# A four-layer graph network on one core: attention scores scaled and summed by one VectorE operation each, row sums moved to GpSimd, one copy in halves

## The chip, the cores and the metric

The kernel runs on one core of a Trainium2 chip. The metric is the time of one execution on the device in microseconds (us), smaller is better. PE is TensorE (the matrix multiplier), PEld its weight loads, DVE is VectorE, ACT is ScalarE, POOL is GpSimd, SP is the engine whose queue issues the DMAs.

## The reference

Input are 128 graphs of 128 nodes with 512 features in fp32, `x` of (128, 128, 512), and one weighted adjacency matrix per graph, `adj` of (128, 128, 128). Four layers follow each other; each adds its result to `x` and normalizes the rows (mean and variance over the 512 features):

```
x = LN(x + relu(An @ x @ W0 + b0))          An = d * (A + I) * d,  d = rowsum(A + I) ** -0.5
qk = x @ Wqk.T ;  q, k = halves of 64
w  = softmax over nodes of ( rowsum( (q @ k.T) / sqrt(64) * A ) )
x = LN(x + w * (x @ Wv.T))
x = LN(x + relu([x, (A @ x) / max(rowsum(A), 1e-6)] @ W2.T))
x = LN(x + An @ (x @ W3 + b3))
```

The second layer matters here. The row sum of masked scores needs no full score matrix: row n of it is the dot product of `q[n]` with `(A @ k)[n]`, over 64 elements, times 1/8. The kernel holds A with its rows divided by `dm = max(rowsum(A), 1e-6)`, so it multiplies by `dm` to undo that. The softmax over the 128 nodes of a graph gives one weight per node.

The fourth layer's bias, seen through An, is `b3` times a row sum of An for each node: `rs = d * (dm * (A_divided @ d) + d)`.

## The kernel before

The 128 graphs are worked in 32 tiles of G = 4 graphs; within a tile a graph's 128 nodes lie on the 128 partitions. Every dense product of a layer (`project`, `l1_out`) is a 2 by 2 block product done with seven instead of eight block products, named B11, T1, B21, T2, B22, T3 and T4 (in this order on PE in layer 3); sums of left-hand blocks are made by `left_sums`, mostly on GpSimd, sums of products on VectorE. In the steady state one turn of the main loop works on two tiles: tile t is in layers 0 and 1, tile u = t - 1 in layers 2 and 3:

```python
        l1_out(t, {})
        l3_agg(u)
        l1_scores(t)
        l3_bias(u)
        l3_out(u, {B11: [lambda: l1_softmax(t)], B21: [lambda: l1_add(t)]})
```

The hooks in braces are called after the named block product. So PE's order is: the products of layer 1 (`p_v`), the four aggregations of layer 3 (`p_agg`, written `agg3` by ACT copies), the four small products of `l1_scores` (`p_sc`, 64 columns for the scores and one for the row sums of each graph), block product B11 of layer 3, the transpose `p_w` of the summed scores, T1, B21, the transpose `p_ws` of the softmax weights back to nodes, then T2, B22 and so on.

Between `p_sc` and `p_ws` stands the softmax. `l1_scores` multiplies on VectorE the PSUM tile `p_sc` by q (two operations of 128 elements into `scr`), sums each graph's 64 products (`w`), and multiplies by 1/8 and `dm` (`w` again). Then it makes `rs` in three operations of 4 elements; `rs` isn't used before `l3_bias` in the next turn. `l1_softmax` transposes `w` on PE to 4 rows of 128, takes the maximum (`mx`), negates it (`nmx`), exponentiates on ACT (`e`, with its sum `ssum`), and normalizes on VectorE (`rsum`, `e`). `l1_add` transposes `e` back (`p_ws`), copies it (`ws`), and adds `ws` times the values to `x`.

`l3_bias` adds `b3` times `rs` to `x` of tile u, one VectorE operation of 512 elements per graph.

The order of the instructions on each engine is not that of the program. The program is recorded as operations in `Plan`; the order on PE is kept, and that of the other four engines is made by a list schedule. It takes, of what is ready, the operation with the earliest due time (counted back from PE's order), with the durations that `estimate` gives. `estimate` also says by a fourth value, `port`, whether an operation may not overlap with another such: every GpSimd operation has it, and VectorE operations with two inputs in SBUF of more than 32 elements. All records have line L271 in the profile, since one line emits every instruction; they are told apart by tile names.

Of the kernel before, what the change touches and what calls it, by code (L numbers as in the profile page):

```python
# [10 lines left out]
FP = mybir.dt.float32  # L11
AF = mybir.ActivationFunctionType
ALU = mybir.AluOpType
AX = mybir.AxisListType

P = 128
K = 32
Q = P // K
G = 4
F = 512  # L20
C = F // P
H = F // 2
ATT = 64
V = H + ATT
# [267 lines left out]
def estimate(engine, method, args, kw):  # L292

    out = args[0]
    n = out.idx.size if isinstance(out, Ref) else 0
    if engine == "tensor":
        return (max(109, 0.85 * n) if method == "transpose" else 2 * max(104, 0.833 * n + (2.5 if n > P else 5))), 100, 0, False
    if method == "dma_start":
        size = max(int(np.prod(v.shape)) if isinstance(v, bass.AP) else v.idx.size * 32 * len(v.quads) for v in args)
        return 470, Plan.LAND + size / 60, size, False  # L300
    if engine == "scalar":
        return (380 if method == "activation" else 160) + 0.83 * n, 0, 0, False
    if engine == "gpsimd":
        return (400 + 150 * n if ALU.pow in args else 250 + 2 * n), 0, 0, True
    if method in ("bn_stats", "tensor_reduce"):
        n = args[1].idx.size
    both = [v for v in args[1:] if isinstance(v, Ref) and v.idx.size == n and v.tile.args[3]["tag"] not in ("pb", "pt")]
    return 160 + (1.12 if len(both) > 1 else 1.04) * n, 0, 0, len(both) > 1 and n > 32


@with_exitstack
def kernel(
# [11 lines left out]
    out: bass.AP,  # L324
):
    nc = Plan(tc.nc, estimate)
    B = x.shape[0]
    NT = B // G
# [5 lines left out]
    tp = Pool(nc, ctx.enter_context(tc.tile_pool(name="tp", bufs=4)), 4)  # L334
    sp = Pool(nc, ctx.enter_context(tc.tile_pool(name="sp", bufs=4)), 4)
# [7 lines left out]
    st = {}  # L343
# [41 lines left out]
    p = ps_t.tile([P, C, P], FP, tag="pt", name="p_warm")  # L385
# [21 lines left out]
    def per_graph(v):  # L407
        return v[:, :, None].to_broadcast([P, G, P])


    def prep_rows(t):
        ana = st["ana", t]
        a = ana[:, 1]
        deg = sp.tile([P, G], FP, tag="deg", name=f"deg_{t}")
        nc.vector.tensor_reduce(deg, a, AX.X, ALU.add)
        dh = sp.tile([P, G], FP, tag="dh", name=f"dh_{t}")
        nc.vector.tensor_scalar(dh, deg, 1.0, None, ALU.add)
        d = sp.tile([P, G], FP, tag="d", name=f"d_{t}")
        nc.gpsimd.tensor_tensor(d, dh, nhalf, ALU.pow)
        dm = sp.tile([P, G], FP, tag="dm", name=f"dm_{t}")  # L420
        nc.vector.tensor_scalar(dm, deg, DEG_EPS, None, ALU.max)
        rdeg = sp.tile([P, G], FP, tag="rdeg", name=f"rdeg_{t}")
        nc.vector.reciprocal(rdeg, dm)
        nc.vector.tensor_tensor(ana[:, 0], a, ident[:, None, :].to_broadcast([P, G, P]), ALU.add)
        nc.vector.tensor_tensor(ana[:, 0], ana[:, 0], per_graph(d), ALU.mult)
        nc.vector.tensor_tensor(ana[:, 1], a, per_graph(rdeg), ALU.mult)
        st["d", t], st["dm", t] = d, dm

    def prep_tiles(t):
        st["anT", t] = ap.tile([P, G, P], FP, tag="anT", name=f"anT_{t}", bufs=3)  # L430
# [29 lines left out]
    def left(name, t):  # L460
        st[name, t] = tp.tile([P, G, C, P], FP, tag="left", name=f"{name}_{t}")

    def aggregate(name, t, g, aT):

        xin = st["x", t]
        p = ps_t.tile([P, C, P], FP, tag="pt", name=f"p_{name}_{t}_{g}")
        with nc.unit():
            for c in range(C):
                nc.tensor.matmul(p[:, c, :], xin[:, g, c * P:(c + 1) * P], aT[:, g, :], start=True, stop=True)
        nc.scalar.copy(st[name, t][:, g], p)  # L470

    def turn_x(name, t, r):

# [26 lines left out]
    def left_sums(name, t, eng=nc.gpsimd, pairs=(slice(0, 2),)):  # L500

        a = st[name, t].rearrange("p (q r) (h c) n -> p q r h c n", r=2, h=2)
        s = [tp.tile([P, 2, 2, P], FP, tag=f"s{i}", name=f"{name}s{i}_{t}", bufs=3) for i in (1, 2, 4)]
        for q in pairs:
            a11, a12, a21, a22 = a[:, q, 0, 0], a[:, q, 0, 1], a[:, q, 1, 0], a[:, q, 1, 1]
            s1, s2, s4 = (v[:, q] for v in s)
            eng.tensor_tensor(s1, a21, a22, ALU.add)
            eng.tensor_tensor(s2, s1, a11, ALU.subtract)
            eng.tensor_tensor(a21, a11, a21, ALU.subtract)
            eng.tensor_tensor(s4, a12, s2, ALU.subtract)  # L510
        st[name, t] = {B11: a[:, :, 0, 0], B21: a[:, :, 0, 1], B22: s[2], T4: a[:, :, 1, 1], T1: s[0], T2: s[1],
                       T3: a[:, :, 1, 0]}
# [170 lines left out]
    def l1_scores(t):  # L683


        d, dm = st["d", t], st["dm", t]
        p = ps_t.tile([P, G, ATT + 1], FP, tag="pt", name=f"p_sc_{t}")
        with nc.unit():
            for g in range(G):
                nc.tensor.matmul(p[:, g, :], st["arT", t][:, g, :], st["v", t][g % 2, 1][:, g // 2, H:V + 1],  # L690
                                 start=True, stop=True)
        w = sp.tile([P, G], FP, tag="w", name=f"w_{t}")
        scr = tp.tile([P, F], FP, tag="row", name=f"scr_{t}", bufs=1)[:, 0:G * ATT].rearrange("p (g a) -> p g a", g=G)
        for r in range(2):
            nc.vector.tensor_tensor(scr.rearrange("p (q r) a -> p q r a", r=2)[:, :, r],
                                    p.rearrange("p (q r) a -> p q r a", r=2)[:, :, r, 0:ATT],
                                    st["v", t][r, 0][:, :, H:V], ALU.mult)
        nc.vector.tensor_reduce(w, scr, AX.X, ALU.add)
        nc.vector.scalar_tensor_tensor(w, w, 1.0 / ATT ** 0.5, dm, ALU.mult, ALU.mult)
        rs = sp.tile([P, G], FP, tag="rs", name=f"rs_{t}")  # L700
        nc.vector.tensor_tensor(rs, p[:, :, ATT], dm, ALU.mult)
        nc.vector.tensor_tensor(rs, rs, d, ALU.add)
        nc.vector.tensor_tensor(rs, rs, d, ALU.mult)
        st["w", t], st["rs", t] = w, rs

    def l1_softmax(t):
        p = ps_t.tile([P, P], FP, tag="pt", name=f"p_w_{t}")
        nc.tensor.transpose(p[:G, :], st.pop(("w", t)), ident)
        mx = sp.tile([G, 1], FP, tag="mx", name=f"mx_{t}")
        nc.vector.tensor_reduce(mx, p[:G, :], AX.X, ALU.max)  # L710
        nmx = sp.tile([G, 1], FP, tag="nmx", name=f"nmx_{t}")
        nc.vector.tensor_scalar(nmx, mx, -1.0, None, ALU.mult)
        e = sp.tile([G, P], FP, tag="e", name=f"e_{t}", bufs=1)
        ssum = sp.tile([G, 1], FP, tag="ssum", name=f"ssum_{t}")
        nc.scalar.activation(e, p[:G, :], AF.Exp, bias=nmx, scale=1.0, accum_out=ssum)
        rsum = sp.tile([G, 1], FP, tag="rsum", name=f"rsum_{t}")
        nc.vector.reciprocal(rsum, ssum)
        nc.vector.tensor_scalar(e, e, rsum, None, ALU.mult)
        st["e", t] = e
# [94 lines left out]
    def l3_agg(t):  # L814
        left("agg3", t)
        for g in (0, 1, 3, 2):
            aggregate("agg3", t, g, st["anT", t])
        left_sums("agg3", t)

    def l3_agg_pair(t, q, eng):  # L820
# [27 lines left out]
    def begin():  # L848

        prep_rows(0)  # L850
        prep_transpose(0)
        weight_sums(w0_sb, nc.gpsimd)
        l0_agg(0, nc.vector, ONE_BY_ONE)
        prep_rows(1)
        l0_out(0, {B21: [lambda: prep_transpose(1)], B22: [lambda: l0_agg(1)]})
        weight_sums(wv_sb, nc.vector)
        for w in (w2x_sb, w2a_sb, w3_sb):
            weight_sums(w, nc.gpsimd)

        l0_out(1)  # L860
        l1_turn(0, turn_on_tensor, (0,))
        finish_tails()
        l1_turn(0, turn_on_tensor, (1,))
        l1_out(0, {T3: [lambda: l1_turn(1, turn_on_tensor)]})
        l1_out(1, {B11: [lambda: l1_scores(0)], T1: [lambda: l1_softmax(0)], B21: [lambda: l1_add(0)]})
        l2_both(0, 0)
        l2_out(0, {B21: [lambda: l2_both(0, 1), lambda: prep(2)], T2: [lambda: l1_scores(1)], B22: [lambda: l1_softmax(1)], T3: [lambda: l1_add(1)]})
        l0_agg(2)
        l2_turn(1)
        l0_out(2, {B21: [lambda: l2_agg(1, 0)], T1: [lambda: l2_agg(1, 1)]})  # L870
        l3_agg(0)
        l3_bias(0)
        l3_out(0)

    def prep(t):
        if t < NT:
            load(t)
            prep_rows(t)
            prep_turn(t)
# [60 lines left out]
```

## Time and profile before

| | |
|---|---|
| time, median of 3 | 2489.15 us (2488.21 to 2489.63) |
| profiled execution | 2489.66 us, of which the profile's span 2487.9 us |
| busy: PE, PEld | 2443.3 us (98%), 2087.7 us (84%) |
| busy: DVE, ACT, POOL | 1792.9 us (72%), 990.7 us (40%), 1302.7 us (52%) |
| one turn of the main loop, 1017.0 to 1093.4 us | 76.4 us, PE busy 75.68 us in it |
| granted TensorE clock | 0.998 |

"Busy" is the time in which an engine has an instruction under way. An idle time is put down in the profile to the instruction whose end released the waiting one. The profile's chain is followed back from the last instruction, each step to what released it. [...]

### The profile page before, as it was taken

How to read it: one execution, taken by the hardware profiler on the slowest of the kernel's cores; microseconds unless marked ns; L12 is line 12 of the kernel's file. 1: busy time of each engine (PE TensorE's matmuls, PEld its weight loads, DVE VectorE, ACT ScalarE, POOL GpSimd, SP SyncE). 2: the span in 40 equal slices, each digit the busy share in tenths (PEclk: the TensorE clock that was granted, in tenths of full speed). 3: DMA queues.
4: the chain of work that ended last, by engine and by line, in shares of the span. 5: the costliest groups of instructions: out<-in, count | busy, mean ns of one | idle time of the engine just before them, and what ended most of it. 6: DMA issues, size and time to landing. Idle time of an engine off the chain costs nothing.

```text
span 2487.9 us, 35407 instructions
## 1 busy us (share of the span) xinstructions
PE 2443.3 (98%) x12462; PEld 2087.7 (84%) x12462; DVE 1792.9 (72%) x3357; ACT 990.7 (40%) x2057; POOL 1302.7 (52%) x1522
## 2 busy tenths in 40 slices
PE   8999999999999999999999999999999999999998
PEld 7788888888888888888888888888888888888886
DVE  6677776877767777677776767767687676877665
ACT  3344334443334443343433444333444334444335
POOL 5365555545455454555554554645555455545443
PEclk9999999999999999999999999999999999999999
DMA  5143234442334423244332444233443334432220
GB/s 174 26 123 80 77 102 110 123 104 61 106 99 123 123 63 100 84 123 123 83 92 82 114 123 107 70 99 94 123 123 72 86 89 123 123 96 64 81 71 34
DMA packets 393265, 241.14 MB, mean 97 GB/s; under 512 B 140416, under 2 KB 358016, under 8 KB 393088
## 3 DMA queue, kind: packets, MB, share of 16 engines
q1 hardware_dynamic: 393088, 238.88, 35.7%
q8 instruction: 99, 1.62, 0.3%
q14 instruction: 78, 0.64, 0.1%
HBM read 126.62 MB, written 112.20 MB: 96 GB/s over the span
## 4 chain that ended last, share of the span: by engine, by line
PE 90%; DVE 7%; ACT 1%; issue 1%; DMA 1%; SPq 0%; POOL 0%; ACTq 0%; POOLq 0%; DVEq 0%
PE p_o L271 55%; PE p_v L271 19%; PE p_agg L271 14%; DVE x L271 2%; DVE rs L271 2%; DVE w L271 1%; PE p_sc L271 1%; DVE scr L271 1%; ACT e L271 1%; DMA x<-in_x_dram 0%; SPq L271 0%; DVE e L271 0%; DVE mx L271 0%; PE p_ws L271 0%; DVE rsum L271 0%
## 5 line engine op out<-in xcount | busy, mean ns | idle before, releaser
L271 PE MATMUL p_o<-w_sb,agg 128*128 128x256 f32 x2048 | 471.5, 380 | 1.7 <-DVE u_o L271 1.0
L271 PEld LDWEIGHTS p_o<-w_sb,agg 128*128 128x128 f32 x2048 | 385.9, 190 | 54.0 <-ACT s_o L271 1.1
L271 ACT COPY agg<-p_agg 128x512 f32<-128x512 f32 x384 | 221.0, 583 | 450.4 <-PE p_agg L271 450.4
L271 PE MATMUL p_v<-wv_sb,xT 128*128 128x320 f32 x1024 | 291.4, 432 | 0.0
L271 DVE TENSOR_TENSOR v<-p_v,v 128x320 f32<-128x320 f32 x316 | 154.7, 490 | 173.2 <-PE p_v L271 172.1
L271 PE MATMUL p_o<-w2x_sb,xT 128*128 128x256 f32 x1024 | 263.3, 379 | 1.7 <-ACT s_o L271 1.1
L271 PE MATMUL p_o<-w2a_sb,agg 128*128 128x256 f32 x1024 | 262.8, 379 | 0.0
L271 PEld LDWEIGHTS p_v<-wv_sb,xT 128*128 128x128 f32 x1024 | 192.1, 190 | 75.9
L271 PEld LDWEIGHTS p_agg<-anT,x 128*128 128x128 f32 x2048 | 238.7, 192 | 6.9 <-DVE anT L271 0.4
L271 PE MATMUL p_agg<-anT,x 128*128 128x128 f32 x2048 | 239.4, 275 | 0.2 <-DVE anT L271 0.2
L271 POOL TENSOR_TENSOR xT1s<-xT 128x512 f32<-128x512 f32 x32 | 45.5, 1423 | 346.0 <-DVE xT L271 230.0
L271 PEld LDWEIGHTS p_o<-w2x_sb,xT 128*128 128x128 f32 x1024 | 194.1, 190 | 32.6 <-ACT s_o L271 1.9
L271 PE MATMUL p_v<-wv_sb,xT1s 128*128 128x320 f32 x768 | 217.4, 433 | 0.1
L271 PEld LDWEIGHTS p_o<-w2a_sb,agg 128*128 128x128 f32 x1024 | 194.6, 190 | 26.4
L271 DVE TENSOR_TENSOR u_o<-p_o,u_o 128x512 f32<-128x512 f32 (+1 forms) x196 | 131.1, 670 | 118.4 <-PE p_o L271 118.2
L271 ACT ACTIVATE x<-x,nmro,rstdo 128x512 f32<-128x512 f32 x257 | 198.7, 809 | 4.3
L271 PE MATMUL p_o<-w2x_sb,xT2s 128*128 128x256 f32 x768 | 197.3, 379 | 1.5 <-DVE xT2s L271 1.5
L271 PE MATMUL p_o<-w2a_sb,agg2s 128*128 128x256 f32 x768 | 197.1, 379 | 0.0
L271 PEld LDWEIGHTS p_v<-wv_sb,xT1s 128*128 128x128 f32 x768 | 145.7, 190 | 57.7 <-POOL xT1s L271 0.6
L271 PE MATMUL p_o<-w_sb,agg0s 128*128 128x256 f32 x768 | 178.6, 382 | 4.3 <-DVE u_o L271 2.7
L271 ACT ACTIVATE nmro<-mro 128x2 f32<-128x2 f32 (+1 forms) x131 | 26.7, 204 | 389.6 <-POOL mro L271 389.6
L271 PE MATMUL p_o<-w_sb,agg3s 128*128 128x256 f32 x744 | 173.8, 383 | 0.0
(144 smaller groups left out, 4426.1 us busy)
## 6 DMA issues: line engine op xcount, KB each, us to landing
x<-in_x_dram SPq DMA_DIRECT2D x31, 1024.0 KB, 5.6
out_dram<-x SPq DMA_DIRECT2D x31, 1024.0 KB, 5.2
xT2s<-x SPq DMA_DIRECT2D x120, 256.0 KB, 2.5
xT2y<-xT2s SPq DMA_DIRECT2D x240, 128.0 KB, 3.3
xT1s<-x SPq DMA_DIRECT2D x120, 256.0 KB, 2.6
xT1y<-xT1s SPq DMA_DIRECT2D x240, 128.0 KB, 3.2
sa<-ana SPq DMA_DIRECT2D x120, 128.0 KB, 3.5
ya<-sa SPq DMA_DIRECT2D x120, 128.0 KB, 2.7
```

What stands on the lines that cost most here:

```text
L271: getattr(getattr(self.nc, op.engine), method)(*[v.real() if isinstance(v, Ref) else v for v in args], **{k: v.real() if isinstance(v, Ref ...
```

## The change

Five edits:

- `l1_scores` makes `w` by four `scalar_tensor_tensor` operations, one per graph, which multiply 64 elements of `p_sc` by a scalar per node and by q, and sum the products in the same instruction (`accum_out`). The scalar is `dmn = -dm / 8`, made for each tile on ACT in `prep_rows`. So `w` is the negative of what it was.
- `l1_softmax` takes the minimum (`mn`) in place of the maximum, and ACT computes exp(mn - w) with scale -1. The negation `nmx` is gone.
- The last two of the three operations on `rs` go to GpSimd.
- `estimate` sets `port` for VectorE operations with two SBUF inputs of any size.
- `l3_agg` copies the aggregation of its last graph (g = 2) from PSUM in two operations of 256 elements in place of one of 512.

```diff
-    return 160 + (1.12 if len(both) > 1 else 1.04) * n, 0, 0, len(both) > 1 and n > 32
+    return 160 + (1.12 if len(both) > 1 else 1.04) * n, 0, 0, len(both) > 1
...
+        dmn = sp.tile([P, G], FP, tag="dmn", name=f"dmn_{t}")
+        nc.scalar.mul(dmn, dm, -1.0 / ATT ** 0.5)
...
-    def aggregate(name, t, g, aT):
+    def aggregate(name, t, g, aT, parts=1):
...
-        nc.scalar.copy(st[name, t][:, g], p)
+        for c in range(0, C, C // parts):
+            nc.scalar.copy(st[name, t][:, g, c:c + C // parts], p[:, c:c + C // parts])
...
-        scr = tp.tile([P, F], FP, tag="row", name=f"scr_{t}", bufs=1)[:, 0:G * ATT].rearrange("p (g a) -> p g a", g=G)
-        for r in range(2):
-            nc.vector.tensor_tensor(scr.rearrange("p (q r) a -> p q r a", r=2)[:, :, r],
-                                    p.rearrange("p (q r) a -> p q r a", r=2)[:, :, r, 0:ATT],
-                                    st["v", t][r, 0][:, :, H:V], ALU.mult)
-        nc.vector.tensor_reduce(w, scr, AX.X, ALU.add)
-        nc.vector.scalar_tensor_tensor(w, w, 1.0 / ATT ** 0.5, dm, ALU.mult, ALU.mult)
+        scr = tp.tile([P, F], FP, tag="row", name=f"scr_{t}", bufs=1)
+        for g in range(G):
+            nc.vector.scalar_tensor_tensor(scr[:, g * ATT:(g + 1) * ATT], p[:, g, 0:ATT], st["dmn", t][:, g:g + 1],
+                                           st["v", t][g % 2, 0][:, g // 2, H:V], ALU.mult, ALU.mult,
+                                           accum_out=w[:, g:g + 1])
         rs = sp.tile([P, G], FP, tag="rs", name=f"rs_{t}")
         nc.vector.tensor_tensor(rs, p[:, :, ATT], dm, ALU.mult)
-        nc.vector.tensor_tensor(rs, rs, d, ALU.add)
-        nc.vector.tensor_tensor(rs, rs, d, ALU.mult)
+        nc.gpsimd.tensor_tensor(rs, rs, d, ALU.add)
+        nc.gpsimd.tensor_tensor(rs, rs, d, ALU.mult)
...
-        mx = sp.tile([G, 1], FP, tag="mx", name=f"mx_{t}")
-        nc.vector.tensor_reduce(mx, p[:G, :], AX.X, ALU.max)
-        nmx = sp.tile([G, 1], FP, tag="nmx", name=f"nmx_{t}")
-        nc.vector.tensor_scalar(nmx, mx, -1.0, None, ALU.mult)
+        mn = sp.tile([G, 1], FP, tag="mn", name=f"mn_{t}")
+        nc.vector.tensor_reduce(mn, p[:G, :], AX.X, ALU.min)
...
-        nc.scalar.activation(e, p[:G, :], AF.Exp, bias=nmx, scale=1.0, accum_out=ssum)
+        nc.scalar.activation(e, p[:G, :], AF.Exp, bias=mn, scale=-1.0, accum_out=ssum)
...
     def l3_agg(t):
-            aggregate("agg3", t, g, st["anT", t])
+            aggregate("agg3", t, g, st["anT", t], 2 if g == 2 else 1)
```

## The prediction

> **What bounds the kernel now.** I read the page's busy shares and its chain first. PE is busy for 2443.3 of 2487.9 us, so all its idle time, start and end included, is 44.6 us. Nothing in this change makes PE's own work shorter, so that is the ceiling. The chain says which engine stands in PE's way:
>
> ```profile
> PE 2443.3 (98%) x12462; PEld 2087.7 (84%) x12462; DVE 1792.9 (72%) x3357; ACT 990.7 (40%) x2057; POOL 1302.7 (52%) x1522
> ...
> PE 90%; DVE 7%; ACT 1%; issue 1%; DMA 1%; SPq 0%; POOL 0%; ACTq 0%; POOLq 0%; DVEq 0%
> ```
>
> DVE carries 7% of the chain although it is no bottleneck by its busy time. The waits of PE alone name the place:
>
> ```profile
> PE p_ws L271 <- DVE e L271: 22.3, 31, 0.7
> PE p_o L271 <- DVE u_o L271: 3.8, 3, 2.7
> PE p_o L271 <- ACT s_o L271: 1.8, 3, 0.7
> ```
>
> Half of PE's idle time is one wait: in 31 of 32 tiles the transpose `p_ws` waits for the softmax weights `e`, never more than 0.73 us. All other waits come a few times, at the start and the end of the program. So in the steady state PE waits for nothing else. The timeline of VectorE in one turn (start, duration, instruction) shows the chain between `p_sc`, which ends at 1043.39, and `p_ws`:
>
> ```profile
> 1043.41 0.49 DVE L271 TENSOR_TENSOR scr<-p_sc,v 128x128 f32<-128x128 f32 x2 [0.91 <-PE p_sc L271]
> 1043.93 0.42 DVE L271 TENSOR_REDUCE w<-scr 128x4 f32<-128x256 f32 x1
> 1044.39 0.61 DVE L271 SCALAR_TENSOR_TENSOR w<-w,dm 128x4 f32<-128x4 f32 x1
> 1044.92 0.15 DVE L271 TENSOR_TENSOR rs<-p_sc,dm 128x4 f32<-128x4 f32 x1
> 1045.11 1.24 DVE L271 TENSOR_TENSOR rs<-rs,d 128x4 f32<-128x4 f32 x1
> 1046.27 1.83 DVE L271 SCALAR_TENSOR_TENSOR x<-b_sb,rs,x 128x512 f32<-128x512 f32 x1
> 1048.02 0.27 DVE L271 TENSOR_REDUCE mx<-p_w 4x1 f32<-4x128 f32 x1
> 1048.33 0.14 DVE L271 TENSOR_SCALAR nmx<-mx 4x1 f32<-4x1 f32 x1
> ```
>
> Two rows stand out: 1.24 us for 4 elements, where the fastest instruction of the same kind took 0.12, and 1.83 us where the fastest took 0.74. GpSimd's timeline tells why:
>
> ```profile
> 1045.06 1.27 POOL L271 TENSOR_TENSOR agg3s<-agg,agg3s 128x512 f32<-128x512 f32 x1
> 1046.28 1.27 POOL L271 TENSOR_TENSOR agg<-agg 128x512 f32<-128x512 f32 x1
> ```
>
> The first ended together with the GpSimd sum beside it (1046.34 and 1046.33), the second, which came as the next sum began, 0.55 us after that sum. And PE's:
>
> ```profile
> 1046.98 1.89 PE L271 MATMUL p_o<-w_sb,agg 128*128 128x256 f32 x8
> 1049.59 0.19 PE L271 MATMUL p_ws<-ident,e 4*128 4x4 f32 x1 [0.72 <-DVE e L271]
> ```
>
> PE is through with B21 at 1048.87 and stands for 0.72 us. `e` ends 6.07 us after `p_sc` here and, by the same timelines, within 0.4 us of that in all turns of the main loop; `p_ws` could go at about 5.3. So the bound is one chain, late by 0.72 us per turn, and its worst part isn't softmax work but `rs` and the bias of another tile, blocked by GpSimd.
>
> **What the Trainium skill says.** "SBUF — State Buffer", section "SBUF: two separate sides": a VectorE instruction with two SBUF inputs and a GpSimd instruction that reads SBUF exclude each other, each for its whole length. The trace agrees (0.12 against 1.24 us); `rs<-p_sc,dm` and `scr`, with one input in PSUM, are not stretched (0.15 and 0.29 us beside a running GpSimd sum). "VectorE: DVE Perf Modes", section "Two Vector instructions with no wait between them": an operation that writes out its accumulator is two instructions, the second an accumulator read. The kernel has none on VectorE; ACT's are listed at 185 to 190 ns. The same page, section on the TRN2 errata, gives (N+151)/0.96 ns for an fp32 `tensor_tensor`: for N = 128 that is 291 ns, and `scr` took 286; for 64 it gives 224 ns.
>
> **The change, part by part**, in times after the end of `p_sc`.
>
> *Scores.* Out go two `scr`, the reduction and the scaling: 0.50 + 0.43 + 0.61 us with gaps, `w` ready at 1.62. In come four operations of 64 elements, each with a PSUM and an SBUF input, so free of the port. One costs at least 0.19 us (`scr`'s pitch of 0.25 less 64 elements at 0.96 GHz) and at most 0.224. The accumulator read isn't in the trace: not below the cheapest VectorE row (MEMSET, 62 ns), since it is an instruction of its own, and I cap it at ACT's 190. So four cost 1.0 to 1.66 us; I take 1.3. That saves 0.3 us (0 to 0.6), but it isn't worth anything by itself: `p_w` follows B11 on PE, at 1.75, and `w` is early enough then as before. It lets VectorE go on sooner.
>
> *Row sums.* Off VectorE go 1.24 us (the first) and 0.14 (the second, which ran beside ACT's exponential). On GpSimd they cost two operations of 4 elements, 0.2 to 0.4 us each (`mro`, `mrv`). GpSimd is idle for 6.8 us after these four sums in the turn shown, and `rs` isn't needed before the next turn. If they stand between the sums, T3's and B22's sums come 0.8 us later; those ended at 1046.33 and 1047.55, and PE wants them from about 1051. Hidden. `rs<-p_sc,dm` stays (0.15).
>
> *The bias in the chain.* `x<-b_sb,rs,x` stays between `w` and `mn`, I assume, with 0.75 us alone and up to 1.83 blocked. It now asks at 1.3 + 0.15 = 1.5 instead of 2.9. `p_w` ends at 2.05; so `mn` starts at 2.2 if the bias isn't blocked, at 3.6 (1.66 + 0.15 + 1.83) if it is.
>
> *Minimum.* `nmx` falls out: 0.17 us. `mn` costs what `mx` did.
>
> From `mn` to `e`: 0.23 + 0.48 (ACT) + 0.18 + 0.31 = 1.2 us, as now. So `e` is ready 3.4 to 4.8 us after `p_sc`, and PE asks for it at 5.3 (0.14 of signalling included). Even a foreign 0.67 us `u_o` in the chain fits at the low end and costs 0.2 us at the high one. The wait goes to zero: 22.3 us.
>
> *`dmn`.* 32 ACT operations of 0.20 us (`nmro`, 204 ns); ACT is idle 60% of the time. Hidden unless it blocks its queue (below).
>
> *Copy in halves.* 128x256 copies took 0.38 us in the last tile (`s_o`), so 0.76 for 0.585: +0.18 us on ACT, which then idles 2.04 us until `s_o`. Its readers gain nothing: GpSimd reads it after its first sum, which ends later (1043.63) than the copy (1043.16), and PE didn't wait for it. Zero; no loss either for that reason.
>
> *Port flag.* It applies to VectorE operations of at most 32 elements with two SBUF inputs of the output's size. Before, those were the scaling of `w` and the two on `rs`. None of them is left on VectorE: the rest of the small ones have one such input, or PSUM. So this edit does nothing by itself; the order changes only through the operations exchanged.
>
> Downstream, all that follows `p_ws` (`ws`, `x`, statistics, the turn by DMA, the transposes `xT2`) starts from it, so it moves along with PE. The `xT2` transposes finish 1.2 to 1.4 us before PE reads them in most turns.
>
> Sum: 22.3 us, against the profiled span 2487.9, plus up to 1 us in the last tile, whose chain runs on through VectorE. That execution took 2489.66, the median is 2489.15. I forecast 2489.15 - 22.65 = 2466.5 us.
>
> **Rivals.** A change within 0.2% (5 us) can't be told from none here.
>
> *A, the wait goes (0.72).* As above: 2463 to 2470.
>
> *B, part of it returns (0.14).* Either four operations with accumulation take over 1.75 us, so that `p_w` waits (in two turns with `w` at 1.97 it waited 0.3), or the order puts another VectorE operation into the chain. For: an unmeasured read. Against: VectorE stood idle before `scr`, so little was pending. 0.1 to 0.5 us in 31 turns: 3 to 15 us back, 2470 to 2482.
>
> *C, no net difference (0.06).* The whole wait moves to `p_w`: the four would need 2.4 us, 0.6 each, twice my cap. Or the order changes in many places. 2484 to 2494.
>
> *D, slower (0.08): `dmn` blocks ACT.* [...] `dmn` needs the degrees of the next tile, for which VectorE waits on the DMA of `adj`:
>
> ```profile
> DVE deg L271 <- DMA ana<-in_adj_dram: 30.6, 17, 3.2
> ```
>
> In the turn shown it landed at 1022.69 and `dm` was there at 1023.89. If `dmn` stands in ACT's queue before the last `agg` copies of `l0_agg` (1017.8 to 1021.1), these wait, the three PSUM buffers of `p_agg` run out at 1019.4, and PE stands for about 5 us. That costs more than all is gained from 5 turns on (22.3 / 5); in half of them it would be 75 - 22, some 2540 us. Against: `dmn` isn't urgent, and the copies are done 1.6 us before the adjacency lands. Behind them stand only copies `v<-p_v`, which have 2.7 us to spare before VectorE reads them at 1027.2.
>
> **How the numbers follow.** Faster takes A and B: 0.86; same 0.06; slower 0.08. The range runs from A's low end less 2 us for unknown gains at the end of the program, 2461, to 2480, most of B: 0.72 and some 0.11.
>
> **What would show it.** Right: PE's waits lack `p_ws <- DVE e`, a turn takes 75.7 us in place of 76.4, the bias is asked for 1.4 us sooner, and PE's idle time is about 22 us. Wrong: a wait of PE at `p_w` for `w` (B), or ACT waiting for DVE `dm` with PE at `p_agg` behind it (D). VectorE accumulator reads over 0.19 us would break the first term.

## The result and the profile after

The changed kernel takes 2458.94 us (median of 4, 2458.5 to 2459.47), beside 2488.68 us for the kernel before: a ratio of 0.9881, 95% interval 0.9864 to 0.9899. That is 29.7 us faster. The forecast was 2466.5 us with a range from 2461 to 2480. The direction and the place were right, but the gain was too small by a quarter, and the measured time lies 2 us below the range. Between the two profiled executions the spans differ by 31.2 us (2487.9 and 2456.7).

The page of the changed kernel, busy shares and chain:

```profile
PE 2436.3 (99%) x12462; PEld 2091.5 (85%) x12462; DVE 1711.2 (70%) x3389; ACT 994.7 (40%) x2120; POOL 1341.0 (55%) x1586
...
PE 97%; DVE 1%; ACT 1%; POOL 0%; DMA 0%; issue 0%; SPq 0%; ACTq 0%; POOLq 0%; DVEq 0%
```

VectorE's share of the chain went from 7% to 1%. Note that PE's busy time fell as well, by 7.0 us, although PE issues the same 12462 matmuls: that is the first sign that "busy" held some waiting before (a part of it is a slower clock at the start, see the last section). The longest wait of PE (in all, times, longest):

```profile
PE p_o L271 <- DVE u_o L271: 3.6, 3, 2.7
```

The row `p_ws <- DVE e` is gone; all that is left belongs to the start and the end of the program. PE in one turn:

```profile
1029.72 1.00 PE L271 MATMUL p_sc<-v,arT 128*128 128x65 f32 x8
1030.57 1.94 PE L271 MATMUL p_o<-w_sb,agg 128*128 128x256 f32 x8
1032.35 0.27 PE L271 MATMUL p_w<-ident,w 128*4 128x128 f32 x1
1032.45 1.89 PE L271 MATMUL p_o<-w_sb,agg3s 128*128 128x256 f32 x8
1034.18 1.89 PE L271 MATMUL p_o<-w_sb,agg 128*128 128x256 f32 x8
1036.01 0.22 PE L271 MATMUL p_ws<-ident,e 4*128 4x4 f32 x1
1036.15 1.13 PE L271 MATMUL p_o<-w_sb,agg3s 128*128 128x256 f32 x4
```

`p_ws` now comes 5.3 us after the end of `p_sc` (1030.72), before it was 6.2. VectorE between the two (the first of four scores with its accumulator read; the other three and `rs` left out):

```profile
1030.77 0.28 DVE L271 SCALAR_TENSOR_TENSOR scr<-p_sc,dmn,v 128x64 f32<-128x64 f32 x1 [0.91 <-PE p_sc L271]
1030.97 0.08 DVE L271 DVE_READ_ACCUMULATOR scr<-p_sc,dmn,v 128x1 f32 x1
...
1032.66 0.28 DVE L271 TENSOR_REDUCE mn<-p_w 4x1 f32<-4x128 f32 x1 [0.91 <-PE p_w L271]
1033.51 0.15 DVE L271 RECIPROCAL rsum<-ssum 4x1 f32<-4x1 f32 x1 [0.57 <-ACT e L271]
1033.69 1.28 DVE L271 TENSOR_SCALAR e<-e,rsum 4x128 f32<-4x128 f32 x1
1034.90 0.67 DVE L271 TENSOR_TENSOR u_o<-p_o,s_o 128x512 f32<-128x512 f32 x1
1035.50 0.73 DVE L271 SCALAR_TENSOR_TENSOR x<-b_sb,rs,x 128x512 f32<-128x512 f32 x1
```

Three things are to be seen. The four scores come every 0.205 us, and the accumulator reads (0.08) lie under the next one, so `w` is ready 0.95 us after `p_sc`. VectorE then waits 0.91 us for `p_w`: the softmax chain waits for PE now, not PE for it. And the bias has moved: it stands behind `u_o`, outside the chain.

**Where the 31.2 us are.** Counted from one `p_ws` to the next, a turn takes 75.49 us in place of 76.40, so 0.91 less, not the 0.72 that the profile showed as idle.

| stretch of the profiled executions | us |
|---|---|
| up to the first `p_ws` (77.49 before, 74.87 after) | 2.6 |
| 28 turns of the main loop, 0.908 each at the median | 25.4 |
| four of these turns were longer still before (76.46 to 76.75) | 0.9 |
| the turns before and after these 28 | 1.9 |
| from the last `p_ws` to the end | 0.4 |

### The profile page after: what moved, and what is told of

Read it like the earlier page. It is cut to its first block, busy times and chain, and to the rows that moved or that the text cites. A ratio compares the mean times of both kernels' runs of the same rounds, so it can differ in the third digit from the quotient of the medians.

```text
span 2456.7 us, 35481 instructions
## 1 busy us (share of the span) xinstructions
PE 2436.3 (99%) x12462; PEld 2091.5 (85%) x12462; DVE 1711.2 (70%) x3389; ACT 994.7 (40%) x2120; POOL 1341.0 (55%) x1586
## 3 DMA queue, kind: packets, MB, share of 16 engines
q8 instruction: 99, 1.62, 0.3%
## 4 chain that ended last, share of the span: by engine, by line
PE 97%; DVE 1%; ACT 1%; POOL 0%; DMA 0%; issue 0%; SPq 0%; ACTq 0%; POOLq 0%; DVEq 0%
PE p_o L271 62%; PE p_v L271 20%; PE p_agg L271 14%; PE p_sc L271 1%; DMA ana<-in_adj_dram 0%; DVE agg0s L271 0%; PE p_ws L271 0%; DVE x L271 0%; PE p_xT L271 0%; ACT xT L271 0%; PE p_w L271 0%; DVE ana L271 0%; ACT x L271 0%; DVE u_o L271 0%; SPq L271 0%
## 5 line engine op out<-in xcount | busy, mean ns | idle before, releaser
L271 ACT COPY agg<-p_agg 128x512 f32<-128x512 f32 (+1 forms) x415 | 222.9, 552 | 456.2 <-PE p_agg L271 456.2
L271 DVE BATCH_NORM_STATS2 bno<-x 128x6 f32<-128x512 f32 x257 | 167.8, 683 | 3.4
```

What stands on the lines that cost most here:

```text
L271: getattr(getattr(self.nc, op.engine), method)(*[v.real() if isinstance(v, Ref) else v for v in args], **{k: v.real() if isinstance(v, Ref ...
```

## Experiments

In what follows a turn is the median distance from one `p_ws` to the next over 28 turns, read from the trace; within a run nearly all turns agree within 0.02 us, so it tells apart what the total times can't. The port is what VectorE operations with two inputs in SBUF and GpSimd operations exclude each other from. An operation is called blocked where it waits for it, as the prediction's row sum that took 1.24 us for 4 elements in place of 0.12, and ended with a GpSimd sum.

| run | time, us (median) | ratio to before (95%) | turn, us |
|---|---|---|---|
| before | 2488.68 | | 76.40 |
| changed | 2458.94 | 0.9881 (0.9864 to 0.9899) | 75.49 |
| `e_rs` | 2465.25 | 0.9899 (0.9884 to 0.9914) | 75.63 |
| `e_scores` | 2459.70 | 0.9880 (0.9864 to 0.9897) | 75.49 |
| `e_min` | 2483.00 | 0.9973 (0.9962 to 0.9984) | 76.23 |
| `e_half` | 2472.52 | 0.9928 (0.9914 to 0.9943) | 75.87 |
| `u_scores` | 2466.26 | 0.9909 (0.9894 to 0.9924) | 75.63 |
| `u_half` | 2460.95 | 0.9890 (0.9874 to 0.9907) | 75.49 |
| `u_rs` | 2459.67 | 0.9884 (0.9869 to 0.9898) | 75.49 |
| `d_late2` | 2471.45 | 0.9931 (0.9916 to 0.9945) | 75.88 |
| `d_late3` | 2485.14 | 0.9987 (0.9981 to 0.9994) | 76.34 |
| `v_start` | 2455.00 | 0.9865 (0.9849 to 0.9882) | 75.49 |

The kernel before ran beside each group: its medians there were 2489.91 us (the four `e_`), 2488.40 (`u_scores`, `u_half`, `d_`) and 2488.30 (`u_rs`, `v_start`).

### One edit alone, on the kernel before

**`e_rs`: only the row sums on GpSimd.**

```diff
-        nc.vector.tensor_tensor(rs, rs, d, ALU.add)
-        nc.vector.tensor_tensor(rs, rs, d, ALU.mult)
+        nc.gpsimd.tensor_tensor(rs, rs, d, ALU.add)
+        nc.gpsimd.tensor_tensor(rs, rs, d, ALU.mult)
```

> The kernel before with one edit: the last two operations on the row sums on GpSimd. Theory (the softmax chain, counted from the end of p_sc, sets the moment of p_ws; PE loses 0.91 us a turn by it, of which 0.16 is hidden at p_w, where w comes too late at 1.62 us): the first blocked row sum leaves the chain, the bias asks for the port at 1.8 in place of 2.9, gets it at 2.95 and ends at 3.7; e is ready at 5.1 and the wait at p_ws goes, but w stays at 1.62, so 0.16 us a turn stay lost: a turn of 75.65 us, about 2465 us, with no wait of PE at p_ws in the profile. Rival 1 (the shown idle time is the whole cost, the rest came from elsewhere): a turn of 75.68, but nothing left that p_w could give, and the changed kernel's 75.49 is reached only by another order. Rival 2 (the bias loses the port to the next sum again): a turn of 76.4, 2488 us.

Measured: a turn of 75.63 us and, but for one of 0.3 us, no wait at `p_ws`. The bias wasn't blocked at all, because it asked just as a GpSimd sum ended (that sum ran from 1035.25 to 1036.52; the next took 1.79 us in place of 1.27), so `e` came at 4.8, sooner than the 5.1 that I had thought. What matters is the 0.14 us that stay lost against 75.49, with no idle time of PE to show for it. PE in that turn:

```profile
1033.92 1.00 PE L271 MATMUL p_sc<-v,arT 128*128 128x65 f32 x8
1034.76 1.95 PE L271 MATMUL p_o<-w_sb,agg 128*128 128x256 f32 x8
1036.68 0.27 PE L271 MATMUL p_w<-ident,w 128*4 128x128 f32 x1
1036.79 1.89 PE L271 MATMUL p_o<-w_sb,agg3s 128*128 128x256 f32 x8
```

and in the kernel before:

```profile
1043.21 1.95 PE L271 MATMUL p_o<-w_sb,agg 128*128 128x256 f32 x8
1045.15 0.27 PE L271 MATMUL p_w<-ident,w 128*4 128x128 f32 x1
1045.25 1.89 PE L271 MATMUL p_o<-w_sb,agg3s 128*128 128x256 f32 x8
```

From the start of B11 to that of T1 are 2.03 us here and 2.04 in the kernel before, but 1.89 in the changed kernel (medians over the turns). `p_w` starts 0.14 us later, yet its row has no bracket with a wait: the record of the matmul in front of it runs on to 1036.71, beyond the start of `p_w`. So in the kernel before 0.15 us a turn were lost at `p_w`, since `w` was ready only at 1.62. That, too, is the port: the scaling `w<-w,dm` took 0.61 us for 4 elements where 0.16 was the least, and in 31 of 32 tiles it ended 0.02 us after a GpSimd sum.

**`e_scores`: only the scores in one operation each** (with `dmn = dm / 8`, so that maximum and negation stay).

```diff
+        dmn = sp.tile([P, G], FP, tag="dmn", name=f"dmn_{t}")
+        nc.scalar.mul(dmn, dm, 1.0 / ATT ** 0.5)
...
+        for g in range(G):
+            nc.vector.scalar_tensor_tensor(scr[:, g * ATT:(g + 1) * ATT], p[:, g, 0:ATT], st["dmn", t][:, g:g + 1],
+                                           st["v", t][g % 2, 0][:, g // 2, H:V], ALU.mult, ALU.mult,
+                                           accum_out=w[:, g:g + 1])
```

> The kernel before with one edit: scores scaled and summed by four operations with an accumulator, with a positive scalar, so maximum and negation stay, as do the row sums on VectorE. Theory: w is ready at 0.95 in place of 1.62 us, and p_w is not late any more; but both row sums now stand ahead of the bias, each finds the port taken (to about 1.6 and 3.0), the bias is blocked to 4.2 and later, and e is ready at about 6 as before. p_ws is set by e, so what p_w gives back is lost at p_ws: a turn of 76.4 us, 2488 us, and the wait shown at p_ws grows to about 0.9 us. Rival 1 (the hidden loss at p_w is a cost of its own): a turn of 76.24, 2484 us. Rival 2 (the chain gets shorter by all that w gains): a turn of 75.7, 2467 us.

This expectation failed: the edit alone gives the whole gain, a turn of 75.49 us and 2459.7 us (one wait of 0.5 us is left at `p_ws`), though both row sums and the bias stand in the chain. VectorE, then GpSimd (`p_sc` ends at 1030.12):

```profile
1031.18 0.76 DVE L271 TENSOR_TENSOR rs<-rs,d 128x4 f32<-128x4 f32 x2
1031.86 1.77 DVE L271 SCALAR_TENSOR_TENSOR x<-b_sb,rs,x 128x512 f32<-128x512 f32 x1
```

```profile
1030.46 1.27 POOL L271 TENSOR_TENSOR agg3s<-agg3s,agg 128x512 f32<-128x512 f32 x1
1031.80 1.27 POOL L271 TENSOR_TENSOR agg3s<-agg,agg3s 128x512 f32<-128x512 f32 x1
1033.04 1.71 POOL L271 TENSOR_TENSOR agg<-agg 128x512 f32<-128x512 f32 x1
```

Since `w` was ready 0.67 us sooner, the first row sum met the end of one GpSimd sum (1031.73) and not the beginning of the next, and both were through by 1031.94. That the second one got in ahead of the next sum, whose record begins at 1031.80, is my reading of it. The bias then waited for one sum, to 1033.07, took the port, and it was GpSimd that was held up (1.71). `e` is ready at 4.86. So 0.67 us earlier at the head of the chain became 1.2 us at its end: here a small shift saved most of the wait for one GpSimd sum of 1.27 us.

**`e_min`: only the sign**, so that the minimum replaces maximum and negation.

```diff
-        nc.vector.scalar_tensor_tensor(w, w, 1.0 / ATT ** 0.5, dm, ALU.mult, ALU.mult)
+        nc.vector.scalar_tensor_tensor(w, w, -1.0 / ATT ** 0.5, dm, ALU.mult, ALU.mult)
...
-        nc.vector.tensor_reduce(mx, p[:G, :], AX.X, ALU.max)
-        nc.vector.tensor_scalar(nmx, mx, -1.0, None, ALU.mult)
+        nc.vector.tensor_reduce(mn, p[:G, :], AX.X, ALU.min)
...
-        nc.scalar.activation(e, p[:G, :], AF.Exp, bias=nmx, scale=1.0, accum_out=ssum)
+        nc.scalar.activation(e, p[:G, :], AF.Exp, bias=mn, scale=-1.0, accum_out=ssum)
```

> The kernel before with one edit: w has the opposite sign, so that the minimum replaces maximum and negation. Theory: e is ready 0.17 us sooner, all of it felt, since the chain sets p_ws: a turn of 76.23 us, 2483.5 us, wait at p_ws 0.55 us. Rival (another order of the list schedule takes it or gives more): a turn that differs from this by over 0.1 us.

Measured: 76.23 us a turn, and PE's waits begin with

```profile
PE p_ws L271 <- DVE e L271: 17.2, 31, 0.6
```

17.2 us over 31 waits are 0.55 each, 0.17 less than before, which is the turn's difference (76.40 - 76.23). This is the cleanest proof that the chain sets `p_ws`: what is taken out of it behind `p_w` comes back one to one.

**`e_half`: only the last aggregation copied in halves.**

```diff
...
-        nc.scalar.copy(st[name, t][:, g], p)
+        for c in range(0, C, C // parts):
+            nc.scalar.copy(st[name, t][:, g, c:c + C // parts], p[:, c:c + C // parts])
...
-            aggregate("agg3", t, g, st["anT", t])
+            aggregate("agg3", t, g, st["anT", t], 2 if g == 2 else 1)
```

> The kernel before with one edit: the last aggregation copied in halves. By the prediction this is worth nothing: 2488.7 us, a turn of 76.4 us. Rival (it acts through the list schedule): in the order of VectorE's instructions the bias now stands behind the softmax, and the second row sum in its place; that row sum is blocked by a sum of GpSimd to about 4.2 us after p_sc, in place of the bias to 4.7, so e comes 0.5 us sooner: a turn of 75.9 us, about 2473 us.

The rival was right: 75.87 us a turn and 2472.5 us, 17 us faster from an edit that I had put at zero. Nobody waited for that copy. It acts through the list schedule: with two shorter copies the planned times shift a little, the second row sum is planned in the place of the bias, and the bias goes behind `u_o`. VectorE in that turn (`p_sc` ends at 1036.75):

```profile
1038.48 2.47 DVE L271 TENSOR_TENSOR rs<-rs,d 128x4 f32<-128x4 f32 x2
1040.87 0.27 DVE L271 TENSOR_REDUCE mx<-p_w 4x1 f32<-4x128 f32 x1
```

Each of the two row sums is now blocked by one GpSimd sum (2.47 us for 8 elements), and that ends at 4.2 us where the bias had ended at 4.7.

### One edit undone, in the changed kernel

**`u_scores`: the scores as before** (two products, a reduction, a scaling with -dm / 8).

```diff
...
-        for g in range(G):
-            nc.vector.scalar_tensor_tensor(..., accum_out=w[:, g:g + 1])
+        for r in range(2):
+            nc.vector.tensor_tensor(...)
+        nc.vector.tensor_reduce(w, scr, AX.X, ALU.add)
+        nc.vector.scalar_tensor_tensor(w, w, -1.0 / ATT ** 0.5, dm, ALU.mult, ALU.mult)
```

> The changed kernel with one edit undone: scores again by two products, a reduction and a scaling with -dm / 8 on VectorE. Theory: e stays early enough (the row sums are on GpSimd), so no wait at p_ws; but w, whose scaling has two SBUF inputs and meets a GpSimd sum that ends at 1.6 us after p_sc, is ready at 1.65 to 1.8 in place of 0.95, and p_w is late by what exceeds 1.48: a turn of 75.65 to 75.8 us, 2463 to 2468 us. Rival (w is worth nothing, as the prediction had it): a turn of 75.49, 2459 us.

Measured: 75.63 us a turn, 2466.3 us and, but for one of 0.3 us, no wait at `p_ws`; `w` was ready at 1.62, a little before the expected span. The same 0.14 us as in `e_rs`, for the same reason.

**`u_half`: the last aggregation copied whole.**

```diff
-            aggregate("agg3", t, g, st["anT", t], 2 if g == 2 else 1)
+            aggregate("agg3", t, g, st["anT", t])
```

> The changed kernel with one edit undone: the last aggregation copied whole. In the order the bias is back between w and the minimum. Theory: with scores and row sums changed, the chain has 1 to 2 us to spare, so it costs nothing: a turn of 75.49 us, 2459 us. Rival (the halves are worth their 14 us of the single edit here too): a turn of 75.9, 2472 us.

Measured: 75.49 us, 2460.95 us with an interval that overlaps the changed kernel's. The bias is back between `w` and `mn` and is blocked there (1.22 us), and nobody notices. The edit that is worth 17 us alone is worth nothing beside the others.

**`u_rs`: the row sums back on VectorE.**

```diff
-        nc.gpsimd.tensor_tensor(rs, rs, d, ALU.add)
-        nc.gpsimd.tensor_tensor(rs, rs, d, ALU.mult)
+        nc.vector.tensor_tensor(rs, rs, d, ALU.add)
+        nc.vector.tensor_tensor(rs, rs, d, ALU.mult)
```

> The changed kernel with one edit undone: the last two row sums back on VectorE. Here the port flag has something to act on: in the order they stand no longer between w and the minimum, but later. Theory: the chain keeps more than 1 us to spare: a turn of 75.49 us and no wait at p_ws, 2459 us. Rival (a blocked row sum is back in the chain or holds up what follows p_ws): a turn above 75.6, over 2462 us.

Measured: 75.49 us, 2459.7 us. With the port flag both operations stand behind `e` in the main loop: in 11 tiles 36 us after `p_sc`, where they take 0.51 us together, in 12 others at 5.4 and 21.6 us (0.30).

The port flag wasn't undone, since there is nothing to run: with and without it, the changed kernel has the same instructions in the same order on all five queues. On the kernel before, where `w<-w,dm` and the two row sums fall under it, it does change the order; what it would be worth there alone was not measured.

### How much of a late `w` is lost, and how much is shown

**`d_late2`, `d_late3`: the changed kernel with two or three copies of `p_sc` to `scr` ahead of the scores**; the scores overwrite them, so nothing else changes.

```diff
+        for _ in range(2):
+            nc.vector.tensor_copy(scr.rearrange("p (g a) -> p g a", g=G)[:, :, 0:ATT], p[:, :, 0:ATT])
         for g in range(G):
```

> The changed kernel with two VectorE copies of 256 elements from p_sc added before the scores; they delay w to about 1.65 to 1.7 us after p_sc and change nothing that is computed. Theory (PE takes p_w at once only if w is ready by 1.48; the first 0.16 us of a delay doesn't show as idle, since it lies under the record of the matmul before): a turn of 75.66 to 75.72 us, about 2465 us, with no wait or one below 0.06 us shown at p_w. Rival (shown idle time is the whole loss): a turn of 75.49 as long as none is shown.

> The same with three copies: w at about 2.0 to 2.05 us. Theory: a turn of 76.0 to 76.06 us, about 2476 us, 0.55 us above the changed kernel's, of which the profile shows 0.36 to 0.42 as waits of PE at p_w, 0.16 less than is lost. Rival: loss and shown wait are equal.

The copies took 0.46 us each, more than expected, so `w` came at 1.86 and 2.32. PE at `p_w`, first for two, then for three copies:

```profile
1038.38 0.27 PE L271 MATMUL p_w<-ident,w 128*4 128x128 f32 x1 [0.23 <-DVE rs L271]
```

```profile
1043.74 0.27 PE L271 MATMUL p_w<-ident,w 128*4 128x128 f32 x1 [0.69 <-DVE rs L271]
```

| | `w` ready, us after `p_sc` | turn less 75.49 | shown as idle | not shown |
|---|---|---|---|---|
| changed | 0.95 | 0 | 0 | |
| `e_rs` | 1.62 | 0.14 | 0 | 0.14 |
| `d_late2` | 1.86 | 0.39 | 0.23 | 0.16 |
| `d_late3` | 2.32 | 0.85 | 0.69 | 0.16 |

The turn grows by what `w` exceeds 1.47 or 1.48 us, and the profile's idle time is 0.16 us less than that in both cases. This is the difference between the record of a 128x256 matmul (0.379 us) and the distance at which they follow each other (1.73 us for eight, 0.216 each): in the changed kernel `p_w` starts 0.16 us before the record in front of it ends. At `p_ws` it is otherwise. There the overlap is 0.07 us when nothing stalls, and what is hidden is 0.04 us in all three kernels that wait there: from B21's start to T2's are 0.76, 0.59 and 0.24 us more than in the changed kernel, and 0.72, 0.55 and 0.20 are shown (before, `e_min`, `e_half`). The theory holds with its size, although the absolute numbers of the expectations were too low because of the dearer copies.

### A further version, with a shorter start

**`v_start`: the changed kernel, with the sums of the first weights on VectorE.**

```diff
-        weight_sums(w0_sb, nc.gpsimd)
+        weight_sums(w0_sb, nc.vector)
```

> The changed kernel, with the sums of the first layer's weights on VectorE in place of GpSimd. At the start of the program four such sums of 1.45 us on GpSimd block VectorE's own (1.45 to 1.75 us each where 0.4 to 0.7 would do), and PE waits 4 us in all between 12 and 26 us. Theory: four sums of 0.7 us more on VectorE, six operations 0.75 to 1.05 us shorter: the first p_ws comes 2 to 3 us sooner, at 72 to 73 us, 2456.5 us. Rival (the stretch is bound by transfers, or the new order loses as much): the first p_ws at 74 to 75 us, no measurable difference.

Measured: 2455.0 us (2454.54 to 2455.12) and the first `p_ws` at 71.41 us, 3.5 earlier than in the changed kernel, with the same turn. Some 0.7 of the 3.5 were there before the edit acts: the first `p_agg` product starts at 8.27 in place of 8.93. It is the same port again, at the start of the program: in the changed kernel four small sums on VectorE took 1.45 us each beside GpSimd's. PE's longest wait for `u_o` is reduced from 2.7 to 0.5 us:

```profile
PE p_o L271 <- DVE u_o L271: 1.3, 3, 0.5
```

It was measured beside the kernel before and not in one group with the changed kernel, and their intervals overlap; the trace speaks for some 2.8 us.

## Where the prediction was right, and which step of it failed

**The bound: right.** One chain, late at one place once a turn. `e_min` shows it one to one.

**The sum: this step failed. Its main term, "The wait goes to zero: 22.3 us", was too small.** I took the 0.72 us that the profile shows as idle for what a turn loses. It loses 0.91: 0.15 at `p_w`, not shown at all, and 0.76 at `p_ws`, of which 0.72 are shown. From B21's start to T2's are 1.97 us in the changed kernel (1034.18 to 1036.15) and 2.73 in the kernel before (1046.98 to the start of this line):

```profile
1049.71 0.48 PE L271 MATMUL p_o<-w_sb,agg3s 128*128 128x256 f32 x1
```

Over 31 tiles 0.91 us are some 28 us. The prediction's own figures disagreed here: it let `p_ws` go at about 5.3 us, and `p_ws` came at 6.2, which is 0.9 and not 0.72. The Trainium skill says why a record can hide a stall: "Perfetto Trace Analysis", section "Tensor Engine Instruction (MATMUL, LD_WEIGHTS)", tells that the end of a TensorE instruction in the profile is an estimate from its size. The trace agrees: the matmul in front of a stall keeps its 0.379 us while the next could start after 0.216, and the two doses show the missing 0.16. The trace did hold a hint of it that I passed over, as idle time of the weight load without a releaser. In the kernel before:

```profile
PEld p_w L271 <- issue: 10.1, 28, 0.5
```

In the changed kernel and in `e_scores` this row is missing; where `w` comes at 1.62 (`e_rs`, `u_scores`) it is there with 11.1 and 10.8 us. It is no more than a hint: the changed kernel has such a row for `p_ws` (10.7 us, 32 times), where `e` is ready 1 us before `p_ws` starts.

**The scores: the size nearly right, the worth wrong.** Four operations took 0.95 us where I took 1.3 from bounds of 1.0 to 1.66. The lower bound wasn't one: the pitch of 0.25 us that it rests on is half of what two `scr` took together, and they start 0.21 apart. The accumulator read is 0.084 us and overlaps. Wrong is the sentence that the saving "isn't worth anything by itself: `p_w` follows B11 on PE, at 1.75, and `w` is early enough then as before". It was PE that was late at 1.75: in the changed kernel `p_w` starts at 1.62. `w` has to be there by 1.47, and it came at 1.62. That is the 0.15 us a turn, and 0.35 more in two turns in which the port delayed `w` to 1.97. I saw the port in the row sum and the bias, and not in the scaling of `w`. Nor did I see that an earlier head of the chain meets the port at another moment: `e_scores` alone gives all.

**The row sums: right.** 1.24 us blocked, the wait gone without them (`e_rs`), their cost on GpSimd hidden (206 ns each at the median, up to 1.16 us).

**The bias in the chain: an assumption that the list schedule didn't keep**, without effect on the time (`u_half`).

**Minimum: right** (0.17 us). **`dmn`: right.** ACT did wait for `dm`, 21.1 us over 13 times and up to 3.1, as rival D had it, but what stood behind had time: PE has no wait at `p_agg` beyond 0.3 us.

**The copy in halves: zero in the changed kernel, as forecast, for an incomplete reason.** I looked only for who reads the copy. Alone it moves 17 us through the order of other instructions. (The two copies took 0.65 us together, not 0.76.)

**The port flag: right** for the changed kernel, and so was its reason. With the row sums on VectorE it does act: it keeps them out of the chain (`u_rs`).

**What isn't from the change.** About 1.5 of the 2.6 us at the start come from the TensorE clock, see below. Without them the profiled executions differ by 29.7 us, as the medians do; that these agree isn't proof, since the clock of the other executions at this point isn't known.

## What to carry to other kernels

The idle time that the profile shows ahead of a matmul can understate a stall, since its record overlaps the one in front when nothing stalls: by 0.16 us at `p_w`, where a stall up to that length shows no idle time at all, and by 0.04 at `p_ws`. So compare start to start with a place where nothing stalls. Several edits of one late chain don't add up: here either of two would have removed the wait at `p_ws`, and a third gave over half of the gain by accident, so the lateness of the chain caps the sum. With a port that two engines exclude each other from, and with an order made by a list schedule, count what moves relative to what, not only what an operation costs.

## What the runs showed of the hardware that was not expected

- An operation with one SBUF tensor can be held up beside GpSimd too. `e<-e,rsum`, 4x128 with one SBUF tensor and a scalar per partition, took 0.274 us in the kernel before, where no GpSimd sum ran beside it, and 1.276 at the median in the changed kernel, where one does (1033.69 to 1034.97, the sum below ending at 1034.89). `estimate` doesn't flag it. "SBUF — State Buffer", section "SBUF: two separate sides", names a second case beside two inputs, an operation in a two-port mode; that this is such a one wasn't tested.

```profile
1033.63 1.26 POOL L271 TENSOR_TENSOR agg<-agg 128x512 f32<-128x512 f32 x1
```

- A VectorE operation that is already waiting when a GpSimd sum ends (`e_scores`, `u_half`), or asks just then (`e_rs`), goes first, and the next GpSimd sum takes 1.6 to 1.8 us in place of 1.27. In the kernel before, the bias came as the next sum began and waited for all of it.
- In 8 of the 12 profiled executions the TensorE clock is halved for 3.41 us after the first 20.48 us at full clock, as here in the kernel before (column after the busy times: 0.86 on the mean of 12 us), not in the changed kernel, `e_scores`, `u_half` and `v_start`. Eight matmuls of 128x256 that begin at 26.21 take 3.47 us there, and 1.99 in the changed kernel: 1.5 us lost. "TensorE: Matmul & The Clock Gate", section "What's actually happening", says that the clock is halved after at least one idle window and gives 3413 ns for the window. The traces agree with the length, but less than a whole window of idle time was enough. Counted in steps of 3.413 us from the moment the clock first became full, the window that ends where the halving begins holds 2.3 to 2.7 us in which PE has no matmul under way, nearly all from one wait of 2.73 us for `u_o`. In the changed kernel, `e_scores` and `u_half` a border between windows cuts this wait in two, and no window before the end of the program has over 1.76 us; in `v_start` the wait is gone. This fits all 12 traces, at the end of the program too, where 2.2 us in a window were followed by the halving; no run was made to vary it.

```profile
24.00:36.00 12.00, 9.79 (x54) 8.87 (x55) 8.83 (x17) 2.34 (x4) 1.98 (x2) 0.86 0.98 265
```
